# Moving transfers between the issuing queues of a two-block convolution kernel

## The chip, the cores and the metric

The kernel runs on one core of one Trainium2 chip. The metric is device time in microseconds, from the first to the last instruction of the program on that core. The time before the change is 2402.37 us, the median of three runs (2398.63 to 2405.48).

## The reference: what is computed

Two bottleneck blocks follow each other on a batch of 16 images of 1024 channels and 32 x 32 pixels, all in float32. The first block puts local self-attention between two 1x1 convolutions; the second is a 3x3 convolution between two 1x1 convolutions.

```python
B, CIN, H, W = 16, 1024, 32, 32          # x: (16, 1024, 32, 32) float32
WIDTH, OUT, HEADS, KS = 256, 1024, 32, 3

# block 0
h = relu(bn(conv1x1(x, w_conv1)))        # 1024 -> 256 channels
q = relu(bn(conv1x1(h, wq))); k = relu(bn(conv1x1(h, wk))); v = bn(conv1x1(h, wv))
kp   = unfold3x3(k) + (pos_h + pos_w)    # 9 neighbours of each pixel
attn = softmax(einsum('bgdhw,bgdkhw->bgkhw', q, kp), over the 9 neighbours)
h = relu(bn(einsum('bgdkhw,bgkhw->bgdhw', unfold3x3(v), attn)))
x = relu(bn(conv1x1(h, w_conv3)) + x)    # 256 -> 1024, with the residual

# block 1
y = relu(bn(conv1x1(x, w1)))             # 1024 -> 256
y = relu(bn(conv3x3(y, w2)))             # 256 -> 256
x = relu(bn(conv1x1(y, w3)) + x)         # 256 -> 1024, with the residual
```

## The kernel before

TensorE does the products. VectorE does the attention (products with the nine neighbours, sums, softmax without the exponentials) and the transforms of the 3x3 convolution, which is done in Winograd form on groups of four images. ScalarE moves results out of PSUM, with scale, shift and relu, and does the exponentials. The engines work on different images at the same time: the order of the stages is a fixed list, and a small model of the two engines' progress, run when the program is built, decides where VectorE's instructions stand between TensorE's.

A transfer is started by an engine's instruction stream. SyncE, ScalarE and GpSimd each have one; an instruction in it that waits holds up all that stand behind it. These are the transfers that the change touches, as they were.

Weights come into a pool of five rooms. A new one is asked for when the last product with an old one has been issued, so it waits for TensorE. The Winograd weights (U) are computed once at the start, stored to DRAM (`uw`), and loaded for each group of four images.

```python
def more_weights():
    key = name, of, half = queue.pop(0)
    t = wpool.tile([P, HW], F32, tag="w", ...)
    ...
    if of[1] == 0 and name == "w1":
        for part in ...:
            nc.sync.dma_start(view[:, part], src[:, part])
    else:
        nc.sync.dma_start(view, src)
    pieces[key] = view
```

Loads of x (for the first convolution), of the residuals s and r, and of the transformed images V (for the Winograd products) go through one list and share a pool of five rooms:

```python
def more_loads():
    while loads and live[0] < CHUNKS + RESULTS - 1:
        kind, b, c = loads[0]
        ...
        if kind == "V":
            src = form_room(b)[c[0], c[1]]...   # written by VectorE's stores of v below
        ...
        (nc.scalar if kind == "x" and b == 0 else nc.gpsimd).dma_start(t, src)
```

The projections q, k and v of an image. The halves of k are written by ScalarE into one padded tile, `kp`, and stored to DRAM by quarter images with their halo rows; then the halves of v go the same way through the same tile, so that v's half can be written only when the store of k's half has read it:

```python
def halo(name, which, func):                 # name: "bnk" for k, "bnv" for v
    room, backs[name] = by_quarter(name, b, HALO, HEAD_DIM)
    for n in range(NW):                      # NW = 2 halves of 128 channels
        norm(inside(kp, n), rows(conv(which, n)), name, n, func)   # ScalarE
        block = kp[:, n]
        nc.sync.dma_start(room[n], AP(block.tensor, ...))
        yield CHUNK
```

From DRAM the four (q, k, the position term and v) come back in VectorE's layout, one head and quarter image a partition. These are called the moves:

```python
def move(name, tag, shape):
    t = apool.tile([P] + shape, F32, tag=tag, ...)      # one room for each tag
    nc.gpsimd.dma_start(t.rearrange("p d w -> p (d w)"), backs[name])
```

The room of the moved v (`bnv`) and the room `e` hold the taps of the 3x3 weights at the start, until the Winograd weights are made from them:

```python
def load_taps(m):
    tag, shape = (("e", [P, KK, JPIX]), ("bnv", [P, HEAD_DIM, HALO]))[m]
    t = apool.tile(shape, F32, tag=tag, name="g")...

def along(m, i, row):                        # in winograd_weights(), twelve times
    t = hpool.tile([P, 2 * HW], F32, tag="h", name="u")     # hpool: five rooms, also h, q, a, y
    ...                                      # sums on VectorE and ScalarE
    nc.sync.dma_start(uw[i, :, :, m]..., t...)
```

Other transfers that stay as they are: the stores of v (VectorE's transformed images) and of the attention's sum `acc`, and the fetch of that sum as `a`, on SyncE; the stores of q, of the position term, of every result (`r` between the blocks, `out` at the end) on GpSimd.

```python
nc.sync.dma_start(room[:, at // 2, ...], u...)          # transform(): v
nc.sync.dma_start(back, acc...)                         # weighted(): a <- acc
nc.sync.dma_start(a[:, n, :]..., summed[b][n])          # fetch_attended(): a <- a
nc.gpsimd.dma_start(to, t)                              # result(): r or out
```

Of the kernel before, what the change touches and what calls it, by code (L numbers as in the profile page):

```python
# [72 lines left out]
def sa_bottleneck_kernel(ctx: ExitStack, tc: tile.TileContext, x, w1t, wqkvt, w3t, u1t, u2t, u3t, params, out):  # L73
    nc = tc.nc
# [25 lines left out]
    queue, pieces, last_use = [], {}, {}  # L100

    def source(name, half):

        if name[0] == "U":
            return uw[int(name[1]), half]
        if name in ("w3", "u3"):
            return ws[name == "u3", half]
        if name[1] == "1":
            src = {"w1": w1t, "u1": u1t}[name].rearrange("(c p) n -> p c n", p=P)
            return src[:, half * NC // 2 : (half + 1) * NC // 2]  # L110
        at = {"wqk": slice(0, 2 * WID), "wv": slice(2 * WID, 3 * WID)}[name]
        return wqkvt.rearrange("(c p) n -> p c n", p=P)[:, :, at]

    def more_weights():

        if not queue:
            return
        key = name, of, half = queue.pop(0)
        t = wpool.tile([P, HW], F32, tag="w", name=f"{name}{half}_{of[0]}")
        src = source(name, half)  # L120
        n, k = src.shape[-1], 1
        for d in src.shape[1:-1]:
            k *= d
        view = t[:, : k * n].rearrange("p (c n) -> p c n", n=n)
        if len(src.shape) == 4:
            view = t.rearrange("p (m j o) -> p m j o", m=NW, j=2)
        if of[1] == 0 and name == "w1":
            for part in (slice(0, 1), slice(1, k)) if half == 0 else (slice(0, k),):
                nc.sync.dma_start(view[:, part], src[:, part])
        else:  # L130
            nc.sync.dma_start(view, src)
        pieces[key] = view

    def done_with(key):
# [180 lines left out]
# [4 lines that stand above are left out]
            late = kind == "r" and b >= B - NK  # L319

            spare = kind == "x" and b < 2 and c >= CHUNKS
            if live[0] >= CHUNKS and not (kind == "x" and b < 2) and not (late and late_rooms):
                return
            if kind == "V":

                if forms.get((b, c[1] == 2), 0) < NK:
                    return
                src = form_room(b)[c[0], c[1]].rearrange("p k j e -> p (k j e)")
            elif kind == "r":
                if (b, c) not in stored:  # L330
                    return
                src = stored[b, c]
            else:
                src = x[b, c * P : (c + 1) * P, :]
            name = f"{kind}_{b}_{c}".translate(str.maketrans(" ,", "__", "()"))
            if late and live[0] >= CHUNKS:
                t = late_of[loads[0]] = late_rooms.pop(0)
                live[0] -= 1
            elif spare:
                t = rpool.tile([P, HW], F32, tag="r", name=name)  # L340
            else:
                t = xpool.tile([P, NK * 2 * PART], F32, tag="x", name=name)
                t = t if kind == "V" else t[:, :HW]

            (nc.scalar if kind == "x" and b == 0 else nc.gpsimd).dma_start(t, src)  # L345
            loaded[loads.pop(0)] = t
            live[0] += 1

# [15 lines left out]
    def piece(name, half):  # L364
        return name, owner[now[0], name, half], half
# [93 lines left out]
    def project(b):  # L459

        h = hidden.pop(b)

        def conv(which, n):
            ps = psum.tile([P, HW], F32, tag="ps", name="ps")
            name, at = ("wqk", which * WID) if which < 2 else ("wv", 0)
            key, at = piece(name, 0), at + n * P
            for m in range(NW):
                for half in range(2):
                    nc.tensor.matmul(  # L469
                        ps[:, halves(half)],  # L470
                        pieces[key][:, m, at : at + P],
                        h[:, m, halves(half)],
                        start=(m == 0),
                        stop=(m == NW - 1),
                    )
            if n == NW - 1 and which:
                done_with(key)
            return ps

        def norm(dst, src, name, n, func):  # L480
            nc.scalar.activation(  # L481
                dst, src, func,
                bias=col(f"L0_conv_{name}_b", n), scale=col(f"L0_conv_{name}_s", n),
            )

        def halo(name, which, func):

            room, backs[name] = by_quarter(name, b, HALO, HEAD_DIM)
            for n in range(NW):
                norm(inside(kp, n), rows(conv(which, n)), name, n, func)  # L490

                block = kp[:, n]
                nc.sync.dma_start(
                    room[n], AP(block.tensor, block.offset, [block.ap[0], [JROWS * PW, NJ], [1, HALO]])
                )
                yield CHUNK

        backs = relaid[b] = {}
        q = hpool.tile([P, NW, HW], F32, tag="h", name=f"q_{b}")
        room, backs["q"] = by_quarter("q", b, JPIX, HEAD_DIM)  # L500

        def positions():

            ps = psum.tile([P, HW], F32, tag="ps", name="ps")
            for half in range(2):
                for n in range(NW):
                    nc.tensor.matmul(  # L507
                        ps[n * G * NPOS : (n + 1) * G * NPOS, halves(half)],
                        pos[:, n].rearrange("p g t -> p (g t)"),
                        q[:, n, halves(half)],  # L510
                        start=True,
                        stop=True,
                    )
            by_offset = zpool.tile([P, HW], F32, tag="z", name="by_offset")
            nc.scalar.activation(by_offset, ps, AF.Identity)

            room, backs["pos"] = by_quarter("pos", b, JPIX, NPOS)
            by_offset = by_offset.rearrange("p (j w) -> p j w", j=NJ)
            for n in range(NW):
                nc.gpsimd.dma_start(room[n], by_offset[n * G * NPOS : (n + 1) * G * NPOS])  # L520

        k = halo("bnk", 1, RELU)
        yield next(k)
        for n in range(NW):
            norm(q[:, n, :], conv(0, n), "bnq", n, RELU)
            nc.gpsimd.dma_start(room[n], q[:, n, :].rearrange("p (j w) -> p j w", j=NJ))
            yield CHUNK
        yield next(k)
        positions()
        side.add(b)  # L530
        written.add(("qk", b))
        relay("qk", b)
        yield 2.5
        for n, cost in enumerate(halo("bnv", 2, AF.Identity)):
            if n:
                written.add(("v", b))
                relay("v", b)
            yield cost
# [11 lines left out]
    def relay(what, b):  # L550

        if not ((what, b) in written and (what, b) in room_for):
            return
        moved, backs = projected.setdefault(b, {}), relaid[b]
        if what == "qk":
            shapes = (("q", "qc", [HEAD_DIM, JPIX]), ("bnk", "bnk", [HEAD_DIM, HALO]), ("pos", "pc", [NPOS, JPIX]))
        else:
            shapes = (("bnv", "bnv", [HEAD_DIM, HALO]),)
        def move(name, tag, shape):
            t = apool.tile([P] + shape, F32, tag=tag, name=f"{tag}_{b}")  # L560
            nc.gpsimd.dma_start(t.rearrange("p d w -> p (d w)"), backs[name])
            moved[name] = t.rearrange("p d (r w) -> p d r w", w=PW) if shape[1] == HALO else t
            if len(moved) in (3, 4):
                come[what, b] = max(side.vector, side.tensor) if b else side.tensor

        for i, shape in enumerate(shapes):
            if b < 2 or i == 0:
                move(*shape)
            else:

                moves.append((side.tensor + GAP * i, lambda shape=shape: move(*shape)))
# [132 lines left out]
    def form_room(b):  # L704
        b -= b % NK
        if b not in form_rooms:
            form_rooms[b] = dram.tile([NI, 3, P, NK, 2, PART], F32, tag=f"v{b}", name="v")
        return form_rooms[b]
# [281 lines left out]
    for text in (  # L990
# [5 lines left out]
        for word in text.split():  # L996
            b, _, of = word[1:].partition(":")
            for letter in "CQV" if word[0] == "P" else word[0]:
                kind = {"C": "conv1", "Q": "qk", "V": "v", "F": "fused", "W": "wino", "U": "u3"}[letter]
# [413 lines left out]
```

## Time and profile before

| | before |
|---|---|
| median of the runs | 2402.37 us |
| span of the profiled run | 2397.5 us |
| TensorE busy | 2365.3 us (99%) |
| VectorE busy | 2163.7 us (90%) |
| ScalarE busy | 935.0 us (39%) |
| GpSimd busy | 465.8 us (19%) |
| moved by DMA | 691.05 MB, mean 288 GB/s |
| of these, from GpSimd's queue | 470.87 MB |
| from SyncE's queue | 214.49 MB |

In the profile PE is TensorE, DVE is VectorE, ACT is ScalarE, POOL is GpSimd and SP is SyncE; a q after the name (SPq) means the engine's instruction stream, which issues transfers. A line of a timeline gives the start, the duration in us, the engine, the line of the kernel, the operation, what it writes and reads, and how many were merged; in brackets stands the idle time before it and what ended it. A line of the list of waits gives who waited for whom: us in total, times, and the longest. TensorE executes each float32 product in two passes, which the profile counts as two matmuls.

In the page's list of transfers the moves of k and v (16 each, 1360 KB) and of q (16, 1024 KB) are issued by GpSimd, the stores of k and v (32 each, 680 KB) by SyncE, and the loads of U (72, 512 KB) by SyncE.

### The profile page before, as it was taken

To read this page: it belongs to the slowest core of one execution; us is meant where nothing else is said; L and a number is where in the kernel's file an instruction comes from. 1 tells how busy PE (TensorE), PEld (TensorE's weight loads), DVE (VectorE), ACT (ScalarE), POOL (GpSimd) and SP (SyncE) were. 2 spreads that over 40 slices of the span, in tenths; PEclk is the share of its full clock that TensorE was granted. 3 is DMA by queue.
4 is the path that set the end of the run, shared out by engine and by line. 5 is a ranking of instruction groups with operands and counts; after the bars stand their busy time and mean duration, and the time that the engine had idled before them with its cause. 6 is when DMAs were issued, how large, how long until landed. Compare 5 with 4: busy or idle time off the path is not lost.

```text
span 2397.5 us, 18521 instructions
## 1 busy us (share of the span) xinstructions
PE 2365.3 (99%) x6112; PEld 1143.9 (48%) x6112; DVE 2163.7 (90%) x1783; ACT 935.0 (39%) x891; POOL 465.8 (19%) x853
## 2 busy tenths in 40 slices
PE   8999999999999999999999999999999999999998
PEld 3444444444466444444466444444466444444843
DVE  4799998999999999998999999999989999875687
ACT  3323242233222574433122574334222553344278
POOL 3111111111111232111111232111111221111222
PEclk9999999999999999999999999999999999999999
DMA  9969686887798998686888998688788896788977
GB/s 358 350 229 313 241 280 227 258 302 250 287 318 264 322 394 317 225 265 222 260 308 290 306 396 304 233 277 282 251 301 301 308 353 223 255 281 268 331 285 294
DMA packets 295999, 691.05 MB, mean 288 GB/s; under 512 B 20064, under 2 KB 166496, under 8 KB 287456
## 3 DMA queue, kind: packets, MB, share of 16 engines
q0 software_dynamic: 118880, 470.87, 54.4%
q1 hardware_dynamic: 175648, 214.49, 28.3%
q10 hardware_dynamic: 1376, 4.51, 0.5%
q8 instruction: 49, 0.80, 0.1%
q14 instruction: 46, 0.38, 0.0%
HBM read 416.09 MB, written 273.70 MB: 288 GB/s over the span
## 4 chain that ended last, share of the span: by engine, by line
PE 92%; DVE 3%; DMA 3%; ACT 1%; issue 1%; ACTq 0%; SPq 0%; DVEq 0%
PE ps L373 36%; PE ps L405 29%; PE ps L469 13%; PE ps L786 9%; PE ps L1219 4%; PE ps L507 1%; DVE acc L646 1%; DVE acc L664 1%; DMA a<-a 1%; DMA bnk<-kp 1%; DMA U<-uw 0%; DMA uw<-u 0%; DMA V__2_8221<-v 0%; DMA v<-v 0%; DVE form L715 0%
## 5 line engine op out<-in xcount | busy, mean ns | idle before, releaser
L405 PE MATMUL ps<-a,w 128*128 128x512 f32 x1024 | 459.6, 594 | 4.3 <-ACT a L690 4.3
L373 PE MATMUL ps<-result,u 128*128 128x512 f32 x1024 | 459.8, 594 | 3.8 <-ACT result L432 3.8
L373 PE MATMUL ps<-x,w 128*128 128x512 f32 x1024 | 444.4, 595 | 6.4 <-DMA x<-in_x_dram 6.4
L646 DVE TENSOR_TENSOR acc<-e,bnv 128x2048 f32<-128x2048 f32 x144 | 327.6, 2283 | 33.6 <-ACT e L628 30.5
L405 PE MATMUL ps<-y,u 128*128 128x512 f32 x768 | 331.1, 592 | 0.0
L589 DVE TENSOR_TENSOR prod<-qc,bnk 128x2048 f32<-128x2048 f32 x144 | 324.0, 2287 | 1.7
L432 ACT ACTIVATE result<-ps,par 128x1024 f32<-128x1024 f32 x128 | 142.6, 1114 | 463.8 <-PE ps L405 395.4
L373 PEld LDWEIGHTS ps<-x,w 128*128 128x128 f32 x1024 | 195.4, 191 | 252.1 <-issue 251.9
L405 PEld LDWEIGHTS ps<-a,w 128*128 128x128 f32 x1024 | 194.8, 191 | 251.2 <-issue 242.5
L373 PEld LDWEIGHTS ps<-result,u 128*128 128x128 f32 x1024 | 194.8, 190 | 250.7 <-issue 238.2
L664 DVE TENSOR_TENSOR acc<-acc 128x2048 f32<-128x2048 f32 x128 | 293.4, 2292 | 4.4
L405 PEld LDWEIGHTS ps<-y,u 128*128 128x128 f32 x768 | 145.9, 190 | 183.3 <-issue 181.5
L469 PE MATMUL ps<-h,wqk 128*128 128x512 f32 x512 | 222.3, 592 | 0.0
L433 POOL DMA_DIRECT2D r<-result x128 | 68.8, 538 | 633.4 <-ACT result L432 618.0
L594 DVE TENSOR_TENSOR prod<-prod 128x2048 f32<-128x2048 f32 (+1 forms) x80 | 166.2, 2078 | 2.5
L469 PEld LDWEIGHTS ps<-h,wqk 128*128 128x128 f32 x512 | 97.2, 190 | 122.6 <-issue 110.0
L1052 ACT ACTIVATE h<-ps,par 128x1024 f32<-128x1024 f32 x32 | 38.6, 1205 | 280.6 <-PE ps L373 280.6
L432 ACT ACTIVATE result<-ps,bn_sh 128x1024 f32<-128x1024 f32 x96 | 106.6, 1112 | 102.5 <-PE ps L405 102.1
L481 ACT ACTIVATE kp<-ps,par 128x1024 f32<-128x1024 f32 x64 | 77.4, 1210 | 156.5 <-PE ps L469 114.6
L396 ACT ACTIVATE ps<-s 128x1024 f32<-128x1024 f32 x128 | 131.2, 1025 | 2.5
L345 POOL DMA_DIRECT2D x<-in_x_dram x120 | 63.8, 532 | 300.5 <-PE ps L373 229.3
L809 ACT ACTIVATE z<-ps 128x1024 f32<-128x1024 f32 x48 | 49.2, 1025 | 178.1 <-PE ps L786 130.4
(375 smaller groups left out, 2671.4 us busy)
## 6 DMA issues: line engine op xcount, KB each, us to landing
s<-in_x_dram POOLq DMA_DIRECT2D x128, 512.0 KB, 6.2
r<-result POOLq DMA_DIRECT2D x128, 512.0 KB, 4.1
out_dram<-result POOLq DMA_DIRECT2D x126, 512.0 KB, 6.4
x<-in_x_dram POOLq DMA_DIRECT2D x120, 512.0 KB, 5.1
r<-r POOLq DMA_DIRECT2D x111, 512.0 KB, 7.1
v<-v SPq DMA_DIRECT2D x96, 408.0 KB, 4.9
U<-uw SPq DMA_DIRECT2D x72, 512.0 KB, 4.1
bnk<-kp SPq DMA_DIRECT2D x32, 680.0 KB, 7.4
```

The costliest lines, as they stand in the source:

```text
L373: nc.tensor.matmul(ps[n][:, halves(half)], wt[:, c % (NC // 2), n * P : (n + 1) * P], src[:, halves(half)], start=(c == first), stop=(c == ...
L396: nc.scalar.activation(ps, loaded.pop((self.kind, self.b, o)), AF.Identity)
L405: nc.tensor.matmul(self.ahead[o][:, halves(half)], pieces[key][:, n, o % (NC // 2) * P :][:, :P], self.src[:, n, halves(half)], start=Fals ...
L432: nc.scalar.activation(to_, ps, RELU, bias=self.shift(o), scale=1.0)
L469: nc.tensor.matmul(ps[:, halves(half)], pieces[key][:, m, at : at + P], h[:, m, halves(half)], start=(m == 0), stop=(m == NW - 1),)
L481: nc.scalar.activation(dst, src, func, bias=col(f"L0_conv_{name}_b", n), scale=col(f"L0_conv_{name}_s", n),)
L589: nc.vector.tensor_tensor(by_row(t[:, two]), by_row(qc), kc[:, :, i : i + JROWS, j : j + W], ALU.mult)
L594: nc.vector.tensor_add(u[:, :, 0:4], u[:, :, 0:4], u[:, :, 4:8])
L646: nc.vector.tensor_tensor(by_row(dst), rows(e[:, k, :]).unsqueeze(1).to_broadcast([P, HEAD_DIM, JROWS, W]), vc[:, :, i : i + JROWS, j : j ...
L664: nc.vector.tensor_add(acc, acc, t)
L786: nc.tensor.matmul(acc[i][:, at, :, n, :], pieces[key][:, m, at, n * P : (n + 1) * P], v[:, at, :, m * (TILES + TR) :][:, :, :TILES], star ...
L1219: nc.tensor.matmul(ps, w, by, start=i in (1, 2, 7) and not (i == 2 and self.end), stop=True, skip_group_check=True)
```

## The change

Each transfer is put into the queue whose other transfers wait for the same engine. What waits for VectorE (moves, whose rooms VectorE frees, and V, which VectorE's stores fill) goes to SyncE. Weights, whose rooms TensorE frees, go to GpSimd, except the first four loads of the program. The stores of k and v go to ScalarE, which has just written them. The aim is that a transfer that could start is not held up by one that waits for another engine. No computation changes, and the rooms stay the same.

```diff
@@ more_weights
         else:
-            nc.sync.dma_start(view, src)
+            (nc.sync if len(pieces) < 4 else nc.gpsimd).dma_start(view, src)
         pieces[key] = view
@@ more_loads
-            (nc.scalar if kind == "x" and b == 0 else nc.gpsimd).dma_start(t, src)
+            if kind == "V":
+                engine = nc.sync
+            else:
+                engine = nc.scalar if kind == "x" and b == 0 else nc.gpsimd
+            engine.dma_start(t, src)
@@ project / halo
                 block = kp[:, n]
-                nc.sync.dma_start(
+                nc.scalar.dma_start(
                     room[n], AP(block.tensor, block.offset, [block.ap[0], [JROWS * PW, NJ], [1, HALO]])
                 )
@@ relay / move
             t = apool.tile([P] + shape, F32, tag=tag, name=f"{tag}_{b}")
-            nc.gpsimd.dma_start(t.rearrange("p d w -> p (d w)"), backs[name])
+            nc.sync.dma_start(t.rearrange("p d w -> p (d w)"), backs[name])
```

## The prediction

> **What bounds the kernel now.** I read the page's first part, then TensorE's waits, then the timelines around each of those waits.
>
> ```profile
> PE 2365.3 (99%) x6112; PEld 1143.9 (48%) x6112; DVE 2163.7 (90%) x1783; ACT 935.0 (39%) x891; POOL 465.8 (19%) x853
> ...
> PE 92%; DVE 3%; DMA 3%; ACT 1%; issue 1%; ACTq 0%; SPq 0%; DVEq 0%
> ```
>
> TensorE is busy 99%, and 92% of the chain that ended last is TensorE. How much idle time is left? The chain gives the matmul's own pace: 64 of 512 columns take 27.47 us (0.429 each), 288 of 256 columns take 62.36 us (0.2165), and the 128 position matmuls take 0.2425 each (8 in 1.94 us). So 4832 x 0.429 + 1152 x 0.2165 + 128 x 0.2425 = 2354 us of the 2397.5. Of the other 43 us, 6.4 lie before the first matmul and 8.5 after the last. That leaves 28 us for all the waits in the middle and the slow first matmuls after a pause. TensorE's list of waits names the larger ones:
>
> ```profile
> PE ps L373 <- DMA x<-in_x_dram: 6.4, 1, 6.4
> PE ps L405 <- ACT a L690: 4.3, 2, 2.9
> PE ps L373 <- ACT result L432: 3.8, 1, 3.8
> PE ps L786 <- issue: 2.3, 1, 2.3
> PE ps L469 <- ACT by_offset L515: 2.2, 1, 2.2
> ```
>
> The change adds and removes no arithmetic, so it can win only from these 28 us, about 1.2%. A new wait has no such ceiling.
>
> **What the Trainium skill says.** "Perfetto Trace Analysis", Tensor Engine Instruction: the end of a matmul is estimated, so busy time is a model. The trace agrees: mean durations are 594 ns where the starts are 429 ns apart, hence my count by pace. "DMA: Bandwidth & Descriptors", Issuing engines are not separate DMA queues: all issuers share the same 16 DMA engines, and spreading issues saves only issuing time. In the first 100 us the trace agrees (DMA share 1.03 and 371 GB/s at 70 to 80 us). Same page, Queues, rings and completion order: each DMA engine takes turns between the rings of the issuers, and consumes one ring in order. The trace fits: a halo store issued at 55.97 behind two 768 KB stores on SyncE landed 12.1 us later, while the median halo store takes 8.8. "TensorE: Matmul & The Clock Gate", What's actually happening: after an idle window the array starts at half clock. The trace agrees: after the 3.8 us wait at 326 us the next three pairs of starts lie 0.42 us further apart.
>
> **What the change removes: one clear wait.** At 312 us ScalarE finished the second half of k, but its halo store stood in SyncE's queue behind two stores of v that wait for VectorE:
>
> ```profile
> 313.86 1.40 SPq L751 DMA_DIRECT2D v<-v  x2
> 315.32 0.60 SPq L131 DMA_DIRECT2D w<-ws  x1
> 316.01 0.39 SPq L493 DMA_DIRECT2D bnk<-kp  x1
> ```
>
> The store landed 12.2 us later, and ScalarE could overwrite kp only then:
>
> ```profile
> 328.33 1.21 ACT L481 ACTIVATE kp<-ps,par 128x1024 f32<-128x1024 f32 x1 [9.18 <-DMA bnk<-kp]
> 329.44 1.10 ACT L432 ACTIVATE result<-ps,par 128x1024 f32<-128x1024 f32 x1
> ```
>
> The matmul at 330.59 waited for that result: 3.8 us, and with the slow restart (3 x 0.42) about 5.2. On ScalarE's own queue the store goes out at 312.2, 3.8 us earlier, and with the median landing of 8.8 us instead of 12.2 it is there at about 321. The wait disappears: **-5.2 us**. The same pattern at 194 us (the store issued at 201.7, 7.5 us late) helps the 2.2 us wait at 208 us, on which more below.
>
> Moving the 64 halo stores costs ScalarE 64 x 0.36 us (the median of their issues) = 23 us, 29.5 as measured with the slower ones. With 935 us busy of 2397 it has room: in the projection of k, q and v it idles 2.2 us before each ACTIVATE. I count 0.
>
> **What it adds: a wait at the start.** The moves of k, v, q and position into VectorE's layout leave GpSimd for SyncE, into the queue of the stores of the Winograd weights (uw). Before, GpSimd stood here, as the change intends to end:
>
> ```profile
> 69.20 0.54 POOL L561 DMA_DIRECT2D pc<-pos  x1
> 86.16 0.53 POOL L561 DMA_DIRECT2D bnv<-bnv  x1 [16.43 <-DVE u L276]
> 86.68 2.66 POOL L345 DMA_DIRECT2D x<-in_x_dram  x5
> ```
>
> and SyncE did not wait for it:
>
> ```profile
> 67.31 0.36 SPq L291 DMA_DIRECT2D uw<-u  x1
> 69.39 0.36 SPq L493 DMA_DIRECT2D bnv<-kp  x1
> 71.84 14.41 SPq L291 DMA_DIRECT2D uw<-u  x4
> ```
>
> In the changed program the order on SyncE is: six uw stores, the moves of q, k and position, two uw stores, the move of v, then the four uw stores that above start at 71.84. The move of v needs both the landed store of v (85.5 above) and the end of VectorE's reads from the same room (85.0). So the first of the four cannot leave before about 86; above it left at 71.8 and landed at 87.3. It matters because the hidden layer of image 1 is written into the room that this store reads:
>
> ```profile
> 83.65 0.42 ACT L277 ACTIVATE u<-g 128x256 f32<-128x256 f32 x1 [2.30 <-DMA uw<-u]
> 87.48 1.21 ACT L1052 ACTIVATE h<-ps,par 128x1024 f32<-128x1024 f32 x1 [3.11 <-PE ps L373]
> 89.20 1.20 ACT L1052 ACTIVATE h<-ps,par 128x1024 f32<-128x1024 f32 x1 [0.51 <-PE ps L373]
> ```
>
> That write starts 0.2 us after the landing at 87.3, so there is no slack, and TensorE's next matmul at 89.0 needs it. How late will it be? The two uw stores behind the move of position leave at about 68.8 instead of 63.8, which makes the last weights about 3 us late, so the move of v leaves at about 88. Behind it the ring carries 1360 KB for that move and 768 KB for the uw store, beside about 1 MB of x loads: 3.1 MB at 390 GB/s (the windows of 80 to 100 us show 398 and 401) is 8 us, and the store lands near 97. The hidden layer is then 9.5 us late, and with the slow restart (1.3) I count **+10.8 us**, with 7 to 15 as the spread.
>
> **Two smaller terms.** The 2.2 us wait at 208 us is of TensorE for ScalarE, which waits for VectorE's attention of image 0. If TensorE arrives 10 us later and VectorE at most 5, it is gone: **-2.3**. In the Winograd stages the weights (U) join GpSimd's queue, behind stores that wait for ScalarE. I put the trace's times into the new order. In the last stage the third U then leaves at 2215.3 instead of 2209.0, with the matmul at 2220.9; it may be up to 6 us late. Elsewhere loads keep 3 us or more (a U needed at 697.8 lands at 694.8). Some of this will be lost, and the earlier stores relieve the crowd there: **+3**. A little less traffic in front of the last attention's fetch (the 4.3 us wait above): -1.
>
> Sum: 10.8 - 5.2 - 2.3 + 3 - 1 = +5.3, so 2402.4 + 5.3 = **2408 us**.
>
> **Rivals.** *A: the queues' coupling was the cost, and the change wins.* GpSimd's 16.4 us above speaks for it, and moves come up to 40 us earlier when only their own inputs count. But after 100 us no gap over 1 us of VectorE is put down to a move, and from 1915 to 2053 us it runs without a gap, so earlier moves don't shorten the end. If the start and the weights cost nothing, -5.2 - 2.3 - 1 is left: about 2394. *B: ScalarE stalls in its new duty.* The build gives the completion semaphores of SyncE and ScalarE out in turns of eight, so a store on ScalarE also waits for the eighth transfer before it, maybe one of VectorE's. In the trace's times that one has landed at least 6.7 us earlier for all 64 stores, so I expect nothing; if shifts eat that, several us each time, 2415 to 2430. *C: weights starve.* On GpSimd some weights that were loaded far ahead leave 20 to 60 us later (one w1 half would land at 1550 instead of 1479, needed at 1565). All still come in time; if landings double in the shared ring, four Winograd stages could lose 5 each, 20 in place of the 3: about 2425.
>
> **Range and chances.** The low end is A with 1 us lost at the start: 2395. The high end takes the start at 15, the gains as above and half of C's 20: 2402.4 + 15 - 8.5 + 10 = 2419, and 3 for the spread of the runs: 2422. The runs before spread from 2398.6 to 2405.5. A gain over 2% (48 us) is more than the 28 us there are: 0.01. A loss over 2% needs B or C in all stages: 0.04. Within 2%: 0.95.
>
> **What would show it.** Right: in the changed profile TensorE waits 8 to 14 us near 89 us for the hidden layer of image 1, ScalarE there waits for uw's landing, and no wait on kp's store stands at 328. Wrong: no wait near 89 us (the uw stores land before 90), new waits of TensorE for U, x or s in the Winograd and fused stages, or ScalarE idle before its DMA issues.

## The result: 25 us slower

| | before | after |
|---|---|---|
| median of the runs on one chip | 2400.72 us (2398.63 to 2405.48) | 2427.51 us (2425.69 to 2431.34) |
| ratio after / before, 95% interval | | 1.0106 [1.0088, 1.0124] |
| span of the profiled run | 2397.5 us | 2424.9 us |
| moved from GpSimd's / SyncE's / ScalarE's queue | 470.87 / 214.49 / 4.51 MB | 440.47 / 200.33 / 49.07 MB |

The loss lies between 21 and 30 us; the prediction had 5. Below, a ratio r stands for (r - 1) x 2402 us, so that kernels measured on different chips can be compared: the change costs 25.5 us.

The engines' busy times, from the page's first part, are as before to within 0.4% for TensorE, VectorE and ScalarE. So most of the 27.4 us of the profiled run are idle time of TensorE; 7.2 us are matmuls that the profile shows as longer:

```profile
PE 2372.5 (98%) x6112; PEld 1146.0 (47%) x6112; DVE 2164.1 (89%) x1783; ACT 936.8 (39%) x891; POOL 489.5 (20%) x874
```

TensorE's list of waits in the changed kernel (who waited for whom, us in total, times, longest) names them. The wait for `result` has grown from 3.8 us, once, to 15.8, five times; the one for `h` is new:

```profile
PE ps L377 <- ACT result L436: 15.8, 5, 7.3
PE ps L473 <- ACT h L1056: 7.9, 1, 7.9
PE ps L377 <- DMA x<-in_x_dram: 6.3, 1, 6.3
PE ps L511 <- ACT q L485: 3.7, 1, 3.7
PE ps L790 <- issue: 3.4, 3, 2.7
```

To see where each microsecond goes, I set every TensorE instruction of the changed kernel beside the same instruction of the kernel before and read how late it starts. Where that lateness jumps, time is lost (the jump holds the wait and the slow matmuls after it):

| time before, us | lateness goes from ... to, us | what TensorE waits for there |
|---|---|---|
| 51 to 55 | -0.5 to 3.3 | q of image 0 |
| 89 to 92 | 3.3 to 14.0 | h of image 1 (the start, predicted) |
| 211 to 224 | 14.0 to 13.1 | wait of before for ScalarE, a little shorter |
| 331 to 335 | 13.1 to 7.4 | the wait of before is gone (predicted) |
| 367 to 369 | 7.4 to 16.9 | `result`, behind the exponentials of image 2 |
| 488 to 489 | 16.9 to 22.8 | `result`, behind `kp` |
| 1622 to 1624 | 22.8 to 25.1 | `result` |
| 1950 to 1952 | 25.1 to 28.1 | `result` |
| 2124 to 2129 | 28.1 to 24.6 | wait of before for the attention's sum, shorter |
| 2221 to end | 24.6 to 27.1 | U, and other small ones; waits of before for V are gone |

**The start is as predicted.** The timeline of SyncE's queue, 60 to 100 us, has the order that the prediction spelled out: the move of v (`bnv`) cannot go before 90.24, and the four uw stores stand behind it. ScalarE (second fence) then writes h of image 1 at 99.02, after 9.44 us of waiting for uw's landing, where it was 87.48 before:

```profile
68.70 0.37 SPq L565 DMA_DIRECT2D pc<-pos  x1
69.17 0.93 SPq L291 DMA_DIRECT2D uw<-u  x2
90.24 0.33 SPq L565 DMA_DIRECT2D bnv<-bnv  x1
90.63 3.12 SPq L291 DMA_DIRECT2D uw<-u  x4
```

```profile
99.02 2.30 ACT L1056 ACTIVATE h<-ps,par 128x1024 f32<-128x1024 f32 x2 [9.44 <-DMA uw<-u]
```

**The wait at 374 us was not predicted.** ScalarE's timeline there:

```profile
377.78 1.06 ACT L632 ACTIVATE e<-e 128x1024 f32<-128x1024 f32 x1 [15.06 <-DVE e L625]
379.18 1.27 ACT L632 ACTIVATE e<-e 128x1280 f32<-128x1280 f32 x1 [0.34 <-DVE e L625]
380.36 1.09 ACT L436 ACTIVATE result<-ps,par 128x1024 f32<-128x1024 f32 x1
```

In the program ScalarE's exponentials of image 2 stand ahead of a `result` whose matmul was done at 367.4, and they run in that order here: they wait 15 us for VectorE, so `result` comes at 380.36 and TensorE stands still. VectorE is late (23 us against the kernel before, while TensorE is only 7.4 late) for two reasons: 14.0 us from the start, and 9 more between 319 and 330 us (time before), where it waits three times, 6.4 us the longest, until stores of its own transformed images (`v<-v`) have landed. The times from issue to landing of two of these, first in the kernel before, then in the changed one (the line of the store, its issues and the landings):

```profile
L751 SPq DMA_DIRECT2D v<-v x2: 359/359/359, 324.2 to 325.2; - x2
...
DMA to landing us min/median/max: 5.4/6.0/6.5
```

```profile
L755 SPq DMA_DIRECT2D v<-v x2: 359/360/360, 341.0 to 342.0; - x2
...
DMA to landing us min/median/max: 11.6/13.4/15.2
```

The same transfers, on the same queue as before, take twice as long. That is what the experiments had to explain.

### The profile page after: what moved, and what is told of

The parts are those of the page before. It is cut to its first block, busy times and chain, and to the rows that moved or that the text cites. A ratio compares the mean times of both kernels' runs of the same rounds, so it can differ in the third digit from the quotient of the medians.

```text
span 2424.9 us, 18470 instructions
## 1 busy us (share of the span) xinstructions
PE 2372.5 (98%) x6112; PEld 1146.0 (47%) x6112; DVE 2164.1 (89%) x1783; ACT 936.8 (39%) x891; POOL 489.5 (20%) x874
## 3 DMA queue, kind: packets, MB, share of 16 engines
q0 software_dynamic: 121200, 440.47, 51.1%
q1 hardware_dynamic: 121552, 200.33, 24.4%
q10 hardware_dynamic: 35168, 49.07, 5.7%
## 5 line engine op out<-in xcount | busy, mean ns | idle before, releaser
L377 PE MATMUL ps<-result,u 128*128 128x512 f32 x1024 | 462.0, 596 | 15.8 <-ACT result L436 15.8
```

The costliest lines, as they stand in the source:

```text
L377: nc.tensor.matmul(ps[n][:, halves(half)], wt[:, c % (NC // 2), n * P : (n + 1) * P], src[:, halves(half)], start=(c == first), stop=(c == ...
```

## The experiments

A name for each theory, as the expectations use them. **S**: the start is nearly the whole cost, and the later waits follow from it. **R**: the split into more queues is the cost, because transfers that share the 16 DMA engines now land later. **W**: the weights on GpSimd are the cost. Each kernel is given by its edit against the one named; all ratios are to the kernel before, measured beside it.

### Undoing parts of the change

Against the changed kernel, the moves of image 0 go back to GpSimd:

```diff
-            nc.sync.dma_start(t.rearrange("p d w -> p (d w)"), backs[name])
+            (nc.sync if b else nc.gpsimd).dma_start(t.rearrange("p d w -> p (d w)"), backs[name])
```

> The changed kernel, but the four moves of image 0 leave from GpSimd as before, so that the stores of the Winograd weights (uw) go out in time. Theory S (the start is the cost: the 9.5 us wait at 92 us and, through VectorE being 14 us late from then on, the 8 us wait at 374 us and the 4.5 us at 504 us): all these waits go, 2401 to 2407 us. Theory R (the split of the rings is the cost, whatever the start: stores of k and v land late, moves all leave at once): only the 9.5 us at 92 go, the waits at 374 and 504 us stay, 2415 to 2419 us. Theory W (the weights in GpSimd's queue are the cost): as R, 2415 to 2419 us.

Measured: 1.0088 [1.0073, 1.0103], 21.1 us. The wait at 92 us is gone, but one of 6.6 us stands at 362 us and one of 2.7 at 489. VectorE's two stores of the fences above still land in 11.4 and 14.0 us. S falls: without its cause, its consequences stay. It fits R (and W), a little above their ranges. The repair gains 4.4 us where the wait had cost 10.8.

Against the changed kernel, the weights go back to SyncE:

```diff
-            (nc.sync if len(pieces) < 4 else nc.gpsimd).dma_start(view, src)
+            nc.sync.dma_start(view, src)
```

> The changed kernel, but the weights leave from SyncE as before, where they now stand behind the moves. Theory W (weights on GpSimd crowd the stores of q and of the results, and come late in the Winograd stages): the waits from 1970 us on and those at 504 us go, 2408 to 2416 us. Theories S and R: the start and image 2 are as in the changed kernel, and weights behind moves that wait for VectorE may be late: 2424 to 2440 us.

Measured: 1.0157 [1.0128, 1.0186], 37.7 us, 12 more than the changed kernel. W falls for the changed kernel, as S and R had it: with the moves on SyncE, weights belong elsewhere. One of its waits, 6.8 us for a U of the last group, comes up again below.

Against the changed kernel, all moves go back to GpSimd:

```diff
-            nc.sync.dma_start(t.rearrange("p d w -> p (d w)"), backs[name])
+            nc.gpsimd.dma_start(t.rearrange("p d w -> p (d w)"), backs[name])
```

> The changed kernel, but all moves leave from GpSimd as before, where weights now stand behind them. Theory S: the start is repaired by this too, 2398 to 2407 us, the same as the kernel with only image 0's moves put back. Theory R (moves that leave the moment VectorE frees their room collide with the stores of k): 5 us or more faster than that kernel, if weights behind the moves are not late. Theory W: weights now stand behind the moves as well, 2420 us or more.

Measured: 1.0054 [1.0037, 1.0071], 13.0 us. This is 8 us better than with image 0's moves alone put back, as R has it, but the time was still far from that of before, in a kernel without any of the moves that R blamed. So something in the three other parts costs 13 us.

### One part alone

Against the kernel before, the 64 stores of k and v leave from ScalarE, and nothing else changes:

```diff
-                nc.sync.dma_start(
+                nc.scalar.dma_start(
                     room[n], AP(block.tensor, ...))
```

> The kernel before, but the 64 stores of k and v leave from ScalarE. My prediction's step: the 3.8 us wait at 326 us with its slow restart goes, nothing else changes, 2395 to 2398 us. Theory S agrees: 2394 to 2398. Theory R: the stores land in 10 to 16 us in a ring of their own instead of some 8, ScalarE waits for them before it can write kp again, and the gain is eaten: 2400 to 2410 us.

Measured: 1.0079 [1.0056, 1.0102], 19.0 us. This is the step for which the prediction had -5.2 from the wait at 326 us and 0 for the rest; the time lies above R's range (2400 to 2410) too. The wait at 326 is gone; the 2.2 us at 208 have grown to 5.6, and new ones stand at 608 (4.6) and 706 (3.6). The one at 608 shows the whole mechanism. VectorE's timeline, with two waits for the landing of `v<-v`, and ScalarE's, with the exponentials ahead of `result`:

```profile
598.46 1.01 DVE L715 SCALAR_TENSOR_TENSOR v<-form 128x816 f32<-128x816 f32 x1 [7.90 <-DMA v<-v]
...
605.42 1.23 DVE L610 TENSOR_TENSOR tree<-e 128x1024 f32<-128x1024 f32 x1 [2.95 <-DMA v<-v]
...
608.33 2.63 DVE L621 TENSOR_TENSOR e<-e,mx 128x1024 f32<-128x1024 f32 x2
```

```profile
609.59 1.06 ACT L628 ACTIVATE e<-e 128x1024 f32<-128x1024 f32 x1 [12.55 <-DVE e L621]
...
612.17 1.10 ACT L432 ACTIVATE result<-ps,par 128x1024 f32<-128x1024 f32 x1
```

Before, the first of these VectorE instructions started at 589.19 after 2.38 us of waiting, and the exponentials at 597.27, before TensorE needed the `result` behind them. The difference is in the landings of the two stores (before, then with the stores of k and v on ScalarE):

```profile
L751 SPq DMA_DIRECT2D v<-v x2: 359/898/1437, 582.3 to 583.4; - x2
...
DMA to landing us min/median/max: 6.8/8.0/9.2
```

```profile
L751 SPq DMA_DIRECT2D v<-v x2: 360/587/814, 586.1 to 587.1; - x2
...
DMA to landing us min/median/max: 12.4/15.3/18.3
```

Two theories are possible now. **I**: ScalarE's 23 us of issuing are the cost. **T**: the stores in a ring of their own take turns with VectorE's. To tell them apart, three kernels against the kernel before. First, only k's stores on ScalarE:

```diff
+                (nc.scalar if name == "bnk" else nc.sync).dma_start(
```

> The kernel before, but only the stores of k (32) leave from ScalarE; those of v stay on SyncE. Theory T (in a ring of their own the stores of k and v take turns with the transformed images that VectorE stores on SyncE and waits for; where only ScalarE's stores moved, two such stores landed 12.4 and 18.3 us after issue at 586 us instead of 6.8 and 9.2, and it was stores of v that flew beside them): the stores at 586 us land in 7 to 10 us again, the wait at 326 us goes, 2394 to 2401 us. Theory I (ScalarE's time to issue is the cost): half of the 19 us, 2406 to 2411 us.

Measured: 1.0011 [1.0003, 1.0020], 2.6 us. At 584 us VectorE's stores land in 6.8 and 11.0 us, and TensorE doesn't wait there. The time lies between the two ranges, 3.6 us above T's and 1.4 below I's, so it decides nothing; the landings are as T had them. What it shows is that k's half alone costs little, and most of the 19 us need v's half.

Second, all 64 stores on GpSimd:

```diff
+                nc.gpsimd.dma_start(
```

> The kernel before, but the 64 stores of k and v leave from GpSimd, into the ring where x, s, r and the moves are. Theory T: no third ring takes turns, VectorE's stores land as in the kernel before or sooner, 2395 to 2404 us; a store of k behind a move that waits for VectorE may cost up to 5 us more. Theory I: ScalarE issues nothing, 2395 to 2400 us too. If leaving earlier is itself the cost, whatever the ring: 2412 us or more.

Measured: 1.0056 [1.0041, 1.0071], 13.4 us. A miss for T as I had put it: no third ring is in play, yet the stores near 586 us land in 9.5 and 18.0 us and TensorE waits 4.1 us at 608, much as with ScalarE. I misses as well: ScalarE issues none of the stores here. The third reading, that leaving earlier is itself the cost, has the time; the intervals of the two other queues overlap.

Third, everything where it was, with an idle ACTIVATE of the length of an issue behind each half:

```diff
+                nc.scalar.activation(pad, AP(block.tensor, block.offset, [block.ap[0], [1, 192]]), AF.Identity)
```

> The kernel before with all transfers where they were, and an additional small ACTIVATE (128x192, some 0.36 us) on ScalarE behind each of the 64 halves of k and v, as long as an issue of a store. It computes nothing that is used. Theory T: ScalarE has the room, 2399 to 2404 us. Theory I (the 23 us of issuing on ScalarE make its results late for TensorE): 2412 to 2420 us, as with the stores themselves on ScalarE.

Measured: 0.9999 [0.9989, 1.0010]. The 64 ACTIVATEs take 23.3 us in the profile and cost nothing. I falls.

So T was amended to **O**: what counts is the order within SyncE's one queue. There, v's half of kp is issued behind VectorE's stores, and lands after them; in any other queue it takes its share of the DMA engines at once, and in the three kernels below both its stores land before the second of VectorE's. The place near 585 us in six kernels (us from issue to landing; the engines are full there, with a DMA share of 1.07 from 580 to 606 us in the kernel before):

| kernel | v's half of kp leaves from | VectorE's two stores land in | the two stores of v's half in | TensorE's wait at 605 to 612 |
|---|---|---|---|---|
| before | SyncE | 6.8, 9.2 | 11.2, 16.4 | none |
| idle ACTIVATEs | SyncE | 6.6, 10.6 | 11.2, 16.1 | none |
| k's half on ScalarE | SyncE | 6.8, 11.0 | 13.1, 17.0 | none |
| both halves on ScalarE | ScalarE | 12.4, 18.3 | 9.8, 11.4 | 4.6 |
| both halves on GpSimd | GpSimd | 9.5, 18.0 | 10.2, 11.0 | 4.1 |
| v's half on ScalarE (below) | ScalarE | 13.5, 18.6 | 10.7, 12.4 | 4.9 |

The bytes of the four stores are the same in each row, and the last of them lands 19 to 22 us after the first is issued; who is served first has changed. Leaving earlier is not it at this place: in the kernel before, the two stores of v's half leave 0.6 and 0.0 us after ScalarE has written them (584.90 after 584.27, 587.35 after 587.33), with both halves on ScalarE 0.0 us after. VectorE's next instruction wants its store within 7 us; v's half of kp is in nobody's way for long: kp is next written at 671.8 in the kernel before, 68 us after the second store of it landed. The Trainium skill, "DMA: Bandwidth & Descriptors", Queues, rings and completion order, says that SyncE and ScalarE each own a ring on the same 16 engines, and that an engine consumes one ring's descriptors in order and switches between rings. The six rows agree: order holds within a queue, and sharing sets in between two.

### O on the smallest scale, and in the changed kernel

Against the kernel before, two of the trace's 1244 transfers move, those of v's half of image 7 (the 963 of the expectation is a miscount):

```diff
+                (nc.scalar if name == "bnv" and b == 7 else nc.sync).dma_start(
```

> The kernel before, but two transfers of its 963 are moved: the two stores of v's half of kp of image 7 leave from ScalarE. Theory O (the order in SyncE's one ring is what counts: there v's half of kp stands behind the transformed images that VectorE stores and must see landed before it goes on; in any other ring it overtakes them): the third and fourth store of the transformed images near 582 us land in 11 to 20 us instead of 6.8 and 9.2, the exponentials of image 4 come 8 to 12 us later, ScalarE's next result stands behind them, and TensorE waits 4 to 6 us near 608 us, with a slow restart of 2 to 3: 2406 to 2411 us. Theory C (many small collisions sum up, no single place matters): 2400 to 2403 us and no wait of TensorE there.

Measured: 1.0018 [1.0006, 1.0030], 4.3 us, at the low edge. In the profiled run the two VectorE stores land in 8.6 and 16.0 us, VectorE's softmax of image 4 comes 6.3 us later, and TensorE waits 1.9 us at 606. The mechanism is there, about half as large as expected in that run, which at 2401.67 us was one of the quickest of 14 (median 2408.80).

Against the kernel before, all of v's half on ScalarE, k's half on SyncE:

```diff
+                (nc.scalar if name == "bnv" else nc.sync).dma_start(
```

> The kernel before, but the 32 stores of v's half of kp leave from ScalarE. Theory O (they overtake VectorE's stores; k's half has no part in it): the whole loss of moving all 64, without the gain at 326 us: 2416 to 2423 us. Theory C (each moved store costs its share): half of it, 2409 to 2413.

Measured: 1.0030 [1.0019, 1.0042], 7.2 us. The wait (4.9 us, at 606) is there, but O missed the size, and C's range (2409 to 2413) has it at its edge. C had k's half cost as much, though: v's half alone costs 7.2, k's alone 2.6, both 19.0. The two don't add, and which coincidence makes the other 9 us I did not isolate.

That k's half has no part in it, as O had it, is not so either. At 200 us SyncE fetches the attention's sum (`a<-a`, twice 512 KB), and in the kernel before the second store of k's half stands behind it in the queue. With k's half on ScalarE the later fetch lands in 9.7 us, with both halves there in 10.7, with both on GpSimd in 12.4, and TensorE waits 4.6 to 6.6 us near 211 us (time before) for what follows the fetch on ScalarE. Where k's half stays (before, idle ACTIVATEs, v's half alone) the later fetch lands in 7.0 to 8.4 us, and the wait is 1.3 to 2.2. With the weights alone on GpSimd, which also stood behind the fetch, it is 12.1 and 6.4 us. So another transfer than VectorE's store can lose its place in the same way; no run isolates this one.

Against the changed kernel, v's half goes back to SyncE:

```diff
-                nc.scalar.dma_start(
+                (nc.scalar if name == "bnk" else nc.sync).dma_start(
```

> The changed kernel, but the 32 stores of v's half of kp leave from SyncE as before. Theory O: VectorE's stores come first again, the wait at 374 us and most of that at 504 go, 12 to 16 us less than the changed kernel: 2411 to 2416 us; the start stays as it is. Theory C: the changed kernel's time within 4 us, 2424 to 2431, as the two halves then stand behind moves that wait for VectorE.

Measured: 1.0042 [1.0022, 1.0062], 10.1 us, as O has it, that is 15.4 less than the changed kernel. The two stores of VectorE that landed in 11.6 and 15.2 us in the changed kernel land in 7.2 and 10.7 us. The waits at 374 and at 504 us are both gone, which in the table of the result had brought 9.5 + 5.9 = 15.4 us. That of 504 us had another immediate cause: ScalarE waited there for a store of k's half, which left at 490.1 between moves that had left at 486 and landed 15.9 us later. With v's half back the moves leave at 494 to 499, and that store, issued at 487.4, lands in 6.1 us.

Both repairs together:

```diff
-                nc.scalar.dma_start(
+                (nc.scalar if name == "bnk" else nc.sync).dma_start(
...
+            (nc.sync if b else nc.gpsimd).dma_start(t.rearrange("p d w -> p (d w)"), backs[name])
```

> The changed kernel, with the four moves of image 0 on GpSimd and the stores of v's half of kp on SyncE, both as before. Theory O: the two repairs add (6.5 us for the start, 12 to 16 for the order): 2403 to 2410 us. Theory C: the start's 6.5 us alone, 2418 to 2424.

Measured: 0.9997 [0.9985, 1.0008]. As O has it, even a little better: the whole loss is gone, with all else of the change in place: weights on GpSimd, V and the later moves on SyncE, k's half on ScalarE. The repairs do more together than apart: that of the start gains 4.4 us in the changed kernel, and 10.8 once v's half is back; why was not isolated. Near 584 us VectorE's stores land in 8.1 and 10.5 us, and in TensorE's list of waits `result` is back to small ones:

```profile
PE ps L377 <- DMA x<-in_x_dram: 6.4, 1, 6.4
PE ps L790 <- issue: 4.1, 2, 3.0
PE ps L511 <- ACT q L485: 3.7, 1, 3.7
PE ps L409 <- ACT a L694: 3.5, 2, 2.3
PE ps L377 <- ACT result L436: 3.3, 3, 1.3
```

The start alone, against the kernel before (four transfers):

```diff
-            nc.gpsimd.dma_start(t.rearrange("p d w -> p (d w)"), backs[name])
+            (nc.gpsimd if b else nc.sync).dma_start(t.rearrange("p d w -> p (d w)"), backs[name])
```

> The kernel before, but the four moves of image 0 leave from SyncE, ahead of the last four stores of the Winograd weights. The prediction's step (the wait near 89 us, 10.8 us, of which the wait at 208 us gives 2.3 back): 2408 to 2413 us. If VectorE's lateness from the start (14 us in the changed kernel, where TensorE was 13 late) makes new waits later on: 2415 us or more.

Measured: 1.0057 [1.0042, 1.0072], 13.7 us (10 to 17). TensorE's timeline has the wait, 11.9 us, and the first matmuls after it are slow (0.6 + 4 x 0.42):

```profile
101.00 5.21 PE L469 MATMUL ps<-h,wqk 128*128 128x512 f32 x6 [11.88 <-ACT h L1052]
```

After it TensorE is 14.5 us late, and 15.6 at the end. My 10.8 us were 3.7 too few here, and of the 2.2 us of waiting at 208 us only 1.2 went, while 1.9 new ones came at 221 (times of before). The range for new waits later on (2415 us or more) has the time, but not the cause: nearly all of it is lost at once.

### U and V

Against the kernel before, the weights alone on GpSimd, with the diff of the change:

> The kernel before, but the weights (except the first four loads) leave from GpSimd; moves, stores of k and v and V as before. Theory T: SyncE's ring has less in it, VectorE's stores land sooner, 2394 to 2404 us, if the weights behind GpSimd's moves come in time. Theory W (weights on GpSimd are a cost of their own): 2410 us or more, with waits of TensorE for weights or of ScalarE for rooms of results.

Measured: 1.0042 [1.0026, 1.0058], 10.1 us, within W's range (2410 us or more), the largest piece one wait of 9.4 us for a U of the last group near 2220 us. In GpSimd's queue that U stands behind a load of V, which waits for VectorE's store:

```profile
2221.00 0.54 POOL L345 DMA_DIRECT2D V__2_8221<-v  x1 [11.43 <-DMA v<-v]
2221.53 1.06 POOL L433 DMA_DIRECT2D out_dram<-result  x2
2222.58 0.54 POOL L131 DMA_DIRECT2D U<-uw  x1
```

With both repairs, U back on SyncE:

```diff
+            (nc.sync if len(pieces) < 4 or name[0] == "U" else nc.gpsimd).dma_start(view, src)
```

> The kernel with both repairs (moves of image 0 on GpSimd, v's half of kp on SyncE), and the 72 Winograd weights U back on SyncE as well; w and u stay on GpSimd. Theory O and the 9.5 us wait for U that the kernel with the weights alone on GpSimd showed at 2220 us: 2 to 6 us less than with the two repairs, 2399 to 2406 us, level with the kernel before. If U on SyncE stands behind VectorE's stores there, no gain over the two repairs: 2405 to 2412 us.

Measured: 1.0042 [1.0026, 1.0057], 10.1 us: 10.8 more than with the two repairs, where I expected a gain. The wait for the same U takes 8.6 us.

Against the kernel before, V alone on SyncE, with the diff of the change:

> The kernel before, but V (the transformed images that VectorE stored, loaded for the Winograd products) leaves from SyncE. Theory O: V is small beside the rest and waits for stores of the same ring, 2400 to 2406 us. If V stands behind U and VectorE's stores so that TensorE waits for it in the Winograd stages: 2408 us or more.

Measured: 1.0027 [1.0020, 1.0034], 6.5 us, in the second range, but TensorE's wait of 8.0 us is for the same U and not for V. SyncE's queue there:

```profile
2211.50 1.79 SPq L755 DMA_DIRECT2D v<-v  x2
2226.35 0.33 SPq L349 DMA_DIRECT2D V__2_8221<-v  x1
2226.74 0.42 SPq L131 DMA_DIRECT2D U<-uw  x1
```

The same load of V waits from 2213.3 to 2226.35, and the U that could go stands behind it. These misses make one rule together:

| kernel | U from | V from | TensorE's wait for this U, us |
|---|---|---|---|
| before | SyncE | GpSimd | 0.4 (then 0.7 and 2.3 for two V) |
| changed | GpSimd | SyncE | 2.7 |
| both repairs | GpSimd | SyncE | 3.0 |
| weights alone | GpSimd | GpSimd | 9.4 |
| V alone | SyncE | SyncE | 8.0 |
| both repairs, U back | SyncE | SyncE | 8.6 |
| changed, weights back | SyncE | SyncE | 6.8 |

The change swaps U and V, so it keeps them apart. Either half of the swap alone costs 6 to 10 us.

## Why the prediction was wrong

**The bound: right.** The arithmetic is unchanged, and what happened is TensorE's waits and the slow matmuls after them. That only 28 us could be won but any number lost was the right warning. (Its sum is 2353.4 us and not 2354, so 28 is nearer 29.)

**The failed step is "Moving the 64 halo stores costs ScalarE 64 x 0.36 us ... I count 0".** For ScalarE's time that was right: 23.3 us of idle ACTIVATEs cost nothing. But I asked only whom a moved store holds up in its new queue, and not whom it overtakes by leaving the old one. I put the trace's times into the new order and so kept the landings of all other transfers as they were, VectorE's stores above all, and with them VectorE's times. In truth those stores went from 5.4 and 6.5 us to 11.6 and 15.2, VectorE lost 9 us at one place, and ScalarE's exponentials carried that to TensorE. The missing term is 15.4 us in the changed kernel (v's half put back). The prediction's sentence that spreading issues saves only issuing time names the gain alone; spreading these 64 over a second queue cost 19.0 us.

**The wait at 326 us, -5.2: its mechanism right, its worth not.** The test is whether it goes where TensorE arrives no later than VectorE. In the changed kernel they arrive 13.1 and 14.0 us late, with both repairs 2.9 and 3.8; both times the wait is gone and TensorE gains 5.8 us. That it is gone with k's half alone shows nothing: TensorE arrives 5.5 us late there, VectorE 1.0, and with the idle ACTIVATEs, where no transfer moved, the wait goes in the same way (5.4 and 2.1). The gain didn't last. With both repairs TensorE is 2.9 us early after it, and the whole comes to 0.9997, not to the 0.9978 that -5.2 us would be. That VectorE, busy 90%, sets the pace at later meeting points would explain this, but it was not tested.

**The start, +10.8: right in place and cause, near in size.** 10.8 us in the profile of the changed kernel, 13.7 timed alone, within the spread of 7 to 15. That the first is exact is luck: TensorE is 14.0 us late after it, as it is (14.5) where only the start moved, but 3.3 of that had been lost at 51 to 55 us, a wait for q that the prediction doesn't have.

**The wait at 208 us, -2.3: wrong.** It rested on VectorE being at most 5 us late; it was 14.0 late from 143 us on, and the wait was still 1.6 of 2.2 us.

**U, +3: right for this U** (2.7 us near 2221), and for the reason given: it left at 2240.20, 24.6 us late, that is 2215.6 in the time of before. With the waits for V that went, the last stretch comes to 2.5. **The last fetch, -1:** -3.3 was measured at 2126 us.

**The rivals.** C (weights starve) did not happen in the changed kernel: 2.7 us is its longest wait for a weight. B has the measured time in its range, and ScalarE as the place, but its cause shows up once only: of the 64 stores one left just when a transfer of VectorE with the same completion semaphore had landed (335.24, issue at 335.32), after 1.0 us of idling; before none of the others does ScalarE idle over 0.3 us. A, the aim of the change, gained nothing: with the two harms taken out the other parts come to 0.9997. The range ended at 2422 because it took the worst of each term that I had listed, and the largest was not in the list.

## What to carry to other kernels

Before a transfer is moved out of a queue, look for what stands ahead of it there: the queue may be giving an urgent transfer precedence over a patient one, and in another queue the patient one takes its share of the DMA engines at once. Where the engines are full, a landing is no constant, so follow the engine that waits for the landing (here VectorE) and whatever stands in order behind it on the next engine (ScalarE's exponentials, then TensorE). And keep two streams apart of which one waits while the other could go, as U and V here.

## What the runs showed of the hardware

Not expected: the same two stores of 408 KB on an unchanged queue took 6.8 and 9.2 us or 12.4 and 18.3, depending on whether 2 x 680 KB stood behind them in their queue or in another one. Moving two of 1244 transfers changed the time by 0.18% [0.06, 0.30]. And 64 additional ACTIVATEs on the engine with 39% load, 23.3 us in all, changed it by less than 0.11% either way.
